# An eight-batch adaLN block on one core: the steps around the FFN's pairs put in another order

## The chip, the cores and the metric

The kernel runs on one core of a Trainium2 chip. The metric is the time of one execution on the device in microseconds (us); a lower one is better. A core has five engines that run side by side, each in the order of its own instructions: PE (TensorE, matrix products; its weight loads are shown apart as PEld), DVE (VectorE), ACT (ScalarE), POOL (GpSimd) and SP (SyncE, which here only issues DMAs). They wait for each other by semaphores. Every tile in PSUM that PE writes lies in a bank of its own out of a pool; a new tile waits until the last reader of the bank's previous tile is through.

## The reference

Everything is float32. x is 8 batches of 1024 rows of 256.

```python
mod = (_silu(L0_c) @ L0_wmod).reshape(L0_c.shape[0], 6, 1, -1)
sa, ca, ga, sb, cb, gb = (mod[:, 0], mod[:, 1], mod[:, 2], mod[:, 3], mod[:, 4], mod[:, 5])
ga = (2 * (ga >= 0) - 1) * jnp.maximum(jnp.abs(ga), 0.25)      # gb alike
h = _layernorm(x) * (1 + ca) + sa
x = x + ga * attn(h)       # softmax((h * w_lhs) @ (h * w_rhs).T) @ h
h = _layernorm(x) * (1 + cb) + sb
x = x + gb * (relu(h @ W1 + b1) @ W2 + b2)
```

## The kernel before

**Tiles and steps.** For each batch b there are eight steps i, one for each tile of 128 rows of queries. A step does part of batch b's attention and, in the same stretch, a part of the FFN of batch b-1 (its first half of 512 rows in steps 0 to 3, its second half in steps 4 to 7), of the preparation of batch b+1, and of the way back of finished FFN rows to memory. The order is written out by hand: the program pins every engine's instructions in the order in which the code issues them (`pin`, line 63), so a call that stands later in the loop stands later in the queue of every engine that it uses. Only a few POOL instructions go through a list (`later`, `spare`, lines 632 to 637).

**Attention.** `direct`(b, i) (line 403) makes row tile i of the scores on PE from `lT` and `rT`, the two scaled "sides" of the transposed input, and ACT copies it to `sc`. `mirror`(b, i) (424) fills the column block from the row block: DVE transposes 32x32 blocks into a tile `T`, and SP moves them through DRAM (`move`, 300: four writes of 32 partitions each to `D_m`, then one read). `row_max` (461) is DVE; `max_turn` (466) puts the maxima into a PSUM tile `pm` by PE; `subtract` (471) is DVE, `exponent` (483) ACT. The step works two tiles ahead: step i runs `direct` and `row_max` of `ahead` = tile i+2, and `subtract` and `exponent` of `late` = tile i+1.

Products with the values are made for pairs of tiles (i, i+1) with seven block products instead of eight. `pair_begin` (539) makes the first two on PE (tile `pp`, 16 products, 1.78 us), ACT copies half of it to `W` (one buffer); `pair_begin_sum` (558) is one addition on DVE; `left_sums` (563) are four on POOL, of 1.27 us; `pair_end` (574) makes the other five products into `pq` and `pr`, and `pair_out` (594) adds up and updates x on DVE, reading `W` last.

**FFN.** `ffn_rstd` (639) and `ffn_norm` (643) normalise on ACT into the single buffer `X`; `ffn_blocks` (676) turns it: two DVE transposes and a `move` (`D_f` written, `X_f` read); `ffn_turn` (682) applies scale and shift. The first layer goes by four pairs c of columns of W1, two in each of steps 0 and 1, or 4 and 5. Of a pair, `pair_products` (723) makes `pa`, `pb` and `pc` on PE and copies `pa` to `kept` on ACT, and in between calls `max_turn`; `pair_sums` (751) is five DVE instructions (L757, L760, L763, L766, L767); `pair_last` (769) is one more product into `pa`, an addition on DVE (L775) and one on POOL (L776); `pair_relu` (780) is two on ACT; `pair_turn` (787) four on POOL. The second layer is `y_first` (803) in steps 2 and 6 and `y_second` (825) in 3 and 7. In `y_first`, PE writes the first half of `ya` and of `yb`, ACT copies the first half of `ya` to `Y`, and PE goes on with the second halves in the same banks. `y_gate`, `y_turn`, `y_add` and `y_out` (846 to 878) scale, turn back through DRAM (`D_y`), add to x and store.

**PSUM.** `pa`, `pb`, `pc`, `pp`, `pq`, `pr`, `ya` to `yd` share four banks (pool `ps_a`); scores have two (`ps_s`), the turned maxima two (`ps_t`).

**The next batch.** `prepare_rstd` (269) and `prepare_norm` (272) normalise on ACT into `xg`; `prepare_blocks` (331) turns it (`D_a`, `X_a`); `prepare_turn_apart` (336) writes a side, `rT` (side 1) or `lT` (side 0), of one half of the rows, two ACT instructions each. `direct`(b+1, 0), the first PE work of step 6, needs `lT` of the first half and `rT` of both.

**SP.** All these moves and the stores are in one queue in the order of the code; the read of a move waits on SP until the writes have landed, and what is behind it waits too. The read of `y_turn` alone is put off behind the next move's read (`read_back`, 296).

The change is in the loop over the steps: in its branch `if first:` (lines 1208 to 1281; steps 0, 1, 4 and 5), in the part behind both branches (1341 to 1369), and in `middle` and `norms` (1106 to 1135).

Of the kernel before, what the change touches and what calls it, by code (L numbers as in the profile page):

```python
# [24 lines left out]
def adaln_block_kernel(  # L25
# [445 lines left out]
    def subtract(b, i):  # L471

        pm = pT_t.pop((b, i))
        pT = work.tile([P, NT, P], F32, tag="pT", name=f"pT_{b}_{i}")
        nc.vector.tensor_tensor(  # L475
            pT.rearrange("p j (a v) -> p j a v", v=V),
            score_columns(b, i),
            pm[:, :P].rearrange("p (j a v) -> p j a v", j=1, v=V).to_broadcast([P, NT, NV, V]),
            ALU.subtract,
        )  # L480
        pT_t[b, i] = pT

    def exponent(b, i):
        nc.scalar.activation(pT_t[b, i], pT_t[b, i], AF.Exp)  # L484
# [78 lines left out]
    def left_sums(b, i):  # L563


        s1 = two_t["s1"] = work.tile([P, TH, P], F32, tag="s1", name=f"s1_{b}_{i}", bufs=1)
        nc.gpsimd.tensor_tensor(s1, *halves(pT_t[b, i + 1]), ALU.add)  # L567
        (a11, a12), (a21, a22) = halves(pT_t[b, i]), halves(pT_t[b, i + 1])
        add = nc.gpsimd.tensor_tensor
        add(a21, a11, a21, ALU.subtract)  # L570
        add(a11, s1, a11, ALU.subtract)
        add(a12, a12, a11, ALU.subtract)
# [91 lines left out]
    def x_plus(b, g):  # L664

        for t in range(g * TH, (g + 1) * TH):
            xr = x_tile(b, t)
            later(xr, xr, rows_t[b][:, 1, :], ALU.add)
# [436 lines left out]

    def middle(b, i):

        if i == 0:
            ffn_norm(b - 1, 1)
        elif i == (6 if b < B - 1 else 5):  # L1110
            ffn_norm(b, 0)

    def norms(b, i):
        if b > 0 and i == 0:
            ffn_blocks(b - 1, 1)
        if b == 0:
            if i == 0:
                prepare_start(1)
        elif b + 1 < B:
            if i == 1:  # L1120
                prepare_start(b + 1)
                prepare_stats(b + 1, 0)
            elif i == 2:
                prepare_blocks(b + 1, 0)
                x_plus(b + 1, 0)
                xg_times(b + 1, 0)
        elif i == 5:

            ffn_blocks(b, 0)
        if b == B - 1:  # L1130
            return
        if i == 6:
            if b == 0:
                ffn_norm(b, 0)
            ffn_blocks(b, 0)
# [7 lines left out]
    for b in range(B):  # L1143
        for i in range(NT):
# [63 lines left out]
            if first:  # L1208

                ub, ug = (b - 1, 0) if i >= TH else (b - 2, 1)  # L1210
                back = i % TH == 0 and ub >= 0
                returned = i % TH == 1 and ub >= 0
                pair_products(fb, fg, c, turn_max)
                if i == 0:
                    ffn_rstd(b - 1, 1)
                if back:
                    y_gate(ub)
                if i == 4:
                    if b + 1 < B:
                        prepare_rstd(b + 1, 1)  # L1220
                if i == TH + 1:
                    pair_relu(c - 1)
                pair_sums(fb, fg, c)
                if (b, i) == (1, 0):
                    subtract(*late)
                if back:
                    y_turn(ub, ug)
                if ahead:
                    mirror(*ahead)
                if i % TH == 1:  # L1230
                    left_sums(b, i - 1)
                pair_last(fb, fg, c)
                if i % TH == 1:
                    pair_turn(c - 1)
                if (b, i) == (B - 1, 5):
                    pair_stats(b, 2)
                if late and i != 4 and (b, i) != (1, 0):
                    subtract(*late)
                pair_products(fb, fg, c + 1, (lambda: max_turn(*extra)) if extra else None)
                if (b, i) == (1, 0):  # L1240
                    exponent(*late)
                    late = None
                if (b, i) == (B - 1, 5):
                    ffn_rstd(b, 0)
                if i == 5:
                    exponent(*late)
                    if b + 1 < B:
                        prepare_turn_apart(b + 1, 1, 1)
                        prepare_turn_apart(b + 1, 1, 0)
                if i == 1:  # L1250
                    exponent(*late)
                elif i == 4 and b + 1 < B:
                    prepare_norm(b + 1, 1)
                    x_plus(b + 1, 1)
                pair_relu(c)
                sides_too = i == 4 and b + 1 < B
                if sides_too:
                    prepare_turn_apart(b + 1, 0, 1)
                if late and i == 0:
                    exponent(*late)  # L1260
                if sides_too:
                    prepare_turn_apart(b + 1, 0, 0)
                middle(b, i)
                pair_sums(fb, fg, c + 1)
                pair_last(fb, fg, c + 1)
                if i == 4:
                    if b + 1 < B:
                        prepare_blocks(b + 1, 1)
                        xg_times(b + 1, 1)
                    weights(*late)  # L1270
                if ahead and ahead != extra:
                    row_max(*ahead)
                if returned:
                    for q in range(2):
                        y_add(ub, ug, q)
                pair_turn(c)
                if i == 0:
                    pair_relu(c + 1)
                if c > 0:
                    pair_relu(c + 1)  # L1280
                    pair_turn(c + 1)
            else:
                half = i % TH - 2
                if i == NT - 2 and b < B - 1:
                    pair_stats(b, 2)
                if i == 2:
                    pair_begin(b, i)
                elif i == 3:
                    turn_max()
                elif i == 6:  # L1290
                    pair_begin(b, i, lambda: (max_turn(*late), weights(*late)))
                else:
                    turn_max()
                    pair_end(b, i - 1)
                    if not ahead:

                        pair_out(b, i - 1)
                        pair_stats(b, i - 1)
                if half:
                    y_second(fb, fg)  # L1300
                else:
                    y_first(fb, fg, turn_max if i == 2 else None)
                if ahead:
                    mirror(*ahead)
                if i == 2 and b + 1 < B:
                    prepare_rstd(b + 1, 0)
                elif i == 6 and b + 1 < B:
                    ffn_rstd(b, 0)
                elif i == NT - 1 and b == B - 1:
                    ffn_rstd(b, 1)  # L1310
                if not half:
                    pair_begin_sum(b, i)
                    if i == 2:
                        weights(*late)
                    left_sums(b, i)
                spare()
                early(b, i)
                if late and half:
                    weights(*late)
                middle(b, i)  # L1320
                if i == 2 and b + 1 < B:
                    load_x(b + 1, 1)
                spare()
                if ahead:
                    row_max(*ahead)
                if half:
                    if i == NT - 1 and ahead:
                        pair_out(b, i - 1)
                    y_second_sums(fb)
                    if i == NT - 1 and b == B - 1:  # L1330
                        y_gate(fb)
                    elif i == 3:
                        pair_stats(b, 0)
                        if b + 1 < B:
                            prepare_stats(b + 1, 1)
                else:
                    y_first_sums()
                    if i == NT - 2:
                        pair_stats(b, 4)
                spare()  # L1340
# [10 lines left out]
            if not first:  # L1351
                for _ in range(4 if half else 1):
                    spare()
            if i in (0, 4):
                pair_begin(b, i)
                pair_begin_sum(b, i)
            elif i in (1, 3, 5):
                pair_end(b, i - 1)
                pair_out(b, i - 1)
            elif i == NT - 1 and ahead:  # L1360
                pair_stats(b, i - 1)
            late = ahead if ahead != extra else None
# [82 lines left out]
```

## Time and profile before

| what | value |
|---|---|
| median of 3 runs | 794.17 us (793.29 to 794.22) |
| the profiled execution's own time | 792.67 us |
| span of its profile | 790.7 us |
| granted TensorE clock, mean | 0.996 |
| one batch (from step 2 to step 2, b=1 to 7) | 95.2, 94.8, 96.4, 95.0, 96.0, 95.1 us |
| of a batch, mean busy: PE, DVE, ACT, POOL | 91.8, 78.1, 47.6, 75.2 us |

The profile is of one execution; its times count from the span's start. The views used are the page (busy time of each engine), the waits (which instruction waited for whom), the timeline (instructions with start, duration, engine, line, operation, out<-in, shapes; in square brackets the idle time of the engine before it and what ended it) and the windows (busy time and clock in given stretches). A timeline line can stand for several instructions in a row (x4). PE's ends are modelled, so PE is read by its starts: a product of 256 columns starts 0.216 us after the one before it when nothing holds it up.

### The profile page before, as it was taken

To read this page: it belongs to the slowest core of one execution; us is meant where nothing else is said; L and a number is where in the kernel's file an instruction comes from. 1 tells how busy PE (TensorE), PEld (TensorE's weight loads), DVE (VectorE), ACT (ScalarE), POOL (GpSimd) and SP (SyncE) were. 2 spreads that over 40 slices of the span, in tenths; PEclk is the share of its full clock that TensorE was granted. 3 is DMA by queue.
4 is the path that set the end of the run, shared out by engine and by line. 5 is a ranking of instruction groups with operands and counts; after the bars stand their busy time and mean duration, and the time that the engine had idled before them with its cause. 6 is when DMAs were issued, how large, how long until landed. Compare 5 with 4: busy or idle time off the path is not lost.

```text
span 790.7 us, 12472 instructions
## 1 busy us (share of the span) xinstructions
PE 758.2 (96%) x4044; PEld 626.3 (79%) x4044; DVE 621.0 (79%) x1358; ACT 374.8 (47%) x695; POOL 576.9 (73%) x686
## 2 busy tenths in 40 slices
PE   8999998999989999899998999999998999989998
PEld 4687787787877788787787878878787877878887
DVE  7896988779886889768898788977888779686833
ACT  4563536534365534735346354553646535242521
POOL 3754776968869597895968959698696987759730
PEclk9999999999999999999999999999999999999999
DMA  8033433345544353444544444335453335224230
GB/s 295 15 108 113 127 105 96 104 135 158 144 114 127 111 173 103 114 128 124 177 110 118 147 147 128 97 110 167 132 149 91 114 116 154 74 61 147 56 104 27
DMA packets 106216, 95.25 MB, mean 120 GB/s; under 512 B 29700, under 2 KB 98848, under 8 KB 106152
## 3 DMA queue, kind: packets, MB, share of 16 engines
q1 hardware_dynamic: 98408, 85.81, 37.1%
q10 hardware_dynamic: 7744, 8.65, 3.4%
q8 instruction: 32, 0.52, 0.3%
q14 instruction: 32, 0.26, 0.1%
HBM read 50.62 MB, written 43.81 MB: 119 GB/s over the span
## 4 chain that ended last, share of the span: by engine, by line
PE 70%; DVE 13%; ACT 8%; issue 5%; DMA 3%; POOL 1%; SPq 0%; DVEq 0%; POOLq 0%; ACTq 0%
PE psc L412 14%; PE pr L588 8%; PE pq L588 7%; PE ya L799 6%; PE yc L799 6%; PE yb L799 6%; PE pa L721 4%; PE po L501 4%; PE pp L549 3%; PE pb L721 3%; PE yd L799 3%; DVE pT L475 2%; DVE f L760 2%; DVE u L757 2%; DVE u L767 2%
## 5 line engine op out<-in xcount | busy, mean ns | idle before, releaser
L412 PE MATMUL psc<-rT,lT 128*128 128x512 f32 (+3 forms) x384 | 134.7, 487 | 0.0
L776 POOL TENSOR_TENSOR f<-f,kept 128x256 f32<-128x256 f32 x64 | 48.5, 757 | 107.4 <-DVE f L766 107.4
L484 ACT ACTIVATE pT<-pT 128x1024 f32<-128x1024 f32 x64 | 67.7, 1058 | 92.8 <-DVE pT L475 92.8
L419 ACT COPY sc<-psc 128x512 f32<-128x512 f32 (+3 forms) x96 | 44.4, 477 | 127.3 <-PE psc L412 113.3
L475 DVE TENSOR_TENSOR pT<-sc,pm 128x1024 f32<-128x1024 f32 x64 | 77.0, 1204 | 30.6 <-PE pm L468 12.5
L412 PEld LDWEIGHTS psc<-rT,lT 128*128 128x128 f32 x384 | 66.0, 191 | 36.7 <-issue 26.1
L463 DVE TENSOR_REDUCE m<-sc 128x1 f32<-128x1024 f32 x64 | 77.3, 1208 | 2.4 <-ACT sc L419 1.8
L588 PE MATMUL pq<-tsum,pT 128*128 128x128 f32 (+1 forms) x448 | 60.4, 278 | 9.3 <-DVE f L760 9.3
L721 PE MATMUL pb<-hs,w1s 128*128 128x256 f32 x256 | 66.8, 384 | 0.7 <-POOL hs L711 0.6
L721 PE MATMUL pc<-hT,w 128*128 128x256 f32 x256 | 65.7, 379 | 0.0
L742 ACT COPY kept<-pa 128x512 f32<-128x512 f32 x64 | 37.5, 586 | 56.5 <-PE pa L721 56.5
L588 PEld LDWEIGHTS pq<-tsum,pT 128*128 128x128 f32 x448 | 54.5, 192 | 11.6 <-DVE f L760 11.6
L549 PEld LDWEIGHTS pp<-xg,pT 128*128 128x128 f32 x448 | 54.3, 192 | 10.2 <-issue 6.0
L549 PE MATMUL pp<-xg,pT 128*128 128x129 f32 x448 | 56.0, 276 | 0.9 <-DVE rs_f L650 0.2
L721 PEld LDWEIGHTS pb<-hs,w1s 128*128 128x128 f32 x256 | 49.1, 193 | 9.0 <-POOL hs L711 1.9
L637 POOL TENSOR_TENSOR x<-x,rows 128x256 f32<-128x256 f32 x64 | 44.5, 730 | 13.3 <-ACT rows L1015 10.2
L721 PEld LDWEIGHTS pc<-hT,w 128*128 128x128 f32 x256 | 48.6, 190 | 6.6
L757 DVE SCALAR_TENSOR_TENSOR u<-pb,cols,kept 128x256 f32<-128x256 f32 x64 | 30.5, 477 | 27.1 <-PE pb L721 21.0
L799 PE MATMUL yc<-f,w2s 128*128 128x256 f32 x224 | 50.7, 379 | 0.0
L782 ACT ACTIVATE f<-f 128x512 f32<-128x512 f32 x64 | 39.9, 623 | 21.1 <-DVE f L775 21.1
L721 PE MATMUL pa<-hT,w1s 128*128 128x256 f32 x128 | 39.5, 394 | 9.1 <-ACT kept L742 9.1
L567 POOL TENSOR_TENSOR s<-pT 128x512 f32<-128x512 f32 x28 | 35.7, 1274 | 16.7 <-ACT pT L484 16.7
(167 smaller groups left out, 1934.7 us busy)
## 6 DMA issues: line engine op xcount, KB each, us to landing
D_f<-T_f SPq DMA_DIRECT2D x60, 128.0 KB, 3.5
X_f<-D_f SPq DMA_DIRECT2D x15, 512.0 KB, 3.6
D_a<-T_a SPq DMA_DIRECT2D x56, 128.0 KB, 2.6
D_y<-T_y SPq DMA_DIRECT2D x56, 128.0 KB, 2.3
Y<-D_y SPq DMA_DIRECT2D x14, 512.0 KB, 4.5
out_dram<-x SPq DMA_DIRECT2D x14, 512.0 KB, 3.0
X_a<-D_a SPq DMA_DIRECT2D x13, 512.0 KB, 3.3
x<-in_L_attn_x_dram ACTq DMA_DIRECT2D x12, 512.0 KB, 3.7
```

Source lines behind the costliest of these rows:

```text
L412: nc.tensor.matmul(psc[:, : hi - lo], lhsT=lT_t[b, i // TH][:, k, ts(i % TH, P)], rhs=rT_t[b, n][:, k, lo - n * HALF : HALF], start=(k == ...
L419: nc.scalar.copy(score_row(b, i)[:, lo // V : hi // V, :], psc[:, : hi - lo].rearrange("p (n v) -> p n v", v=V),)
L463: nc.vector.tensor_reduce(m, score_row(b, i), AX.XY, ALU.max)
L475: nc.vector.tensor_tensor(pT.rearrange("p j (a v) -> p j a v", v=V), score_columns(b, i), pm[:, :P].rearrange("p (j a v) -> p j a v", j=1, ...
L484: nc.scalar.activation(pT_t[b, i], pT_t[b, i], AF.Exp)
L549: nc.tensor.matmul(out, lhsT=lhs[:, t, :], rhs=xg_t[b][:, h * TH + t, P : P + XS], start=(t == 0), stop=(t == TH - 1),)
L588: nc.tensor.matmul(out, lhsT=lhs[:, t, :], rhs=rhs[:, t, :], start=(t == 0), stop=(t == TH - 1),)
L637: queue.append(lambda: nc.gpsimd.tensor_tensor(out, in0, row, op))
L721: nc.tensor.matmul(out, lhsT=lhsT, rhs=rhs, start=True, stop=True)
L757: nc.vector.scalar_tensor_tensor(u, pb[:, lo], b1_col(c), kept[:, lo], ALU.add, ALU.add)
L776: nc.gpsimd.tensor_tensor(f[:, c + NH, hi], f[:, c + NH, hi], kept[:, hi], ALU.add)
L799: nc.tensor.matmul(out, lhsT=lhs(c), rhs=rhs(c), start=(c == 0), stop=(c == NH - 1))
```

## The change

- `ffn_norm`(b-1, 1) and `ffn_blocks`(b-1, 1), the second FFN half's normalising and turning, go from step 0 to step 1: the normalising behind both pairs' sums and the exponent, the turning ahead of the next batch's statistics.
- In steps 0, 1 and 5 `subtract` and `exponent` of the late tile, which stood ahead of the second pair's sums, stand behind them. In step 4 they come the other way, from behind everything to directly behind the first pair's sums (`subtract`) and the second pair's products (`exponent`).
- `pair_begin` and `pair_begin_sum` of tiles 4 and 5 go from the end of step 4 to its head, ahead of the FFN's products; in step 0 `pair_begin` stands ahead of the softmax steps, its sum stays at the end. `left_sums`(b, 4) goes from step 5 to step 4.
- The next batch's sides of the first half (four ACT instructions) go from step 4 to the end of step 3; those of the second half go in step 5 from the middle to behind the softmax steps.
- `pair_relu`(1) goes from the end of step 0 to step 1. In step 4 the next batch's turning stays ahead of the row maximum.

```diff
     def middle(b, i):
-        if i == 0:
+        if i == 1:
             ffn_norm(b - 1, 1)
...
     def norms(b, i):
-        if b > 0 and i == 0:
+        if b > 0 and i == 1:
             ffn_blocks(b - 1, 1)
...
+                if i == 4:
+                    pair_begin(b, i)
+                    pair_begin_sum(b, i)
                 pair_products(fb, fg, c, turn_max)
...
-                if i == TH + 1:
+                if i % TH == 1:
                     pair_relu(c - 1)
                 pair_sums(fb, fg, c)
                 if (b, i) == (1, 0):
+                    subtract(*late)
+                elif i == 4:
                     subtract(*late)
                 if back:
                     y_turn(ub, ug)
                 if ahead:
                     mirror(*ahead)
-                if i % TH == 1:
-                    left_sums(b, i - 1)
+                if i == 1:
+                    left_sums(b, 0)
                 pair_last(fb, fg, c)
...
-                if late and i != 4 and (b, i) != (1, 0):
-                    subtract(*late)
                 pair_products(fb, fg, c + 1, (lambda: max_turn(*extra)) if extra else None)
...
-                if i == 5:
+                if i == 4:
                     exponent(*late)
+                    left_sums(b, i)
                     if b + 1 < B:
-                        prepare_turn_apart(b + 1, 1, 1)
-                        prepare_turn_apart(b + 1, 1, 0)
-                if i == 1:
-                    exponent(*late)
-                elif i == 4 and b + 1 < B:
-                    prepare_norm(b + 1, 1)
-                    x_plus(b + 1, 1)
+                        prepare_norm(b + 1, 1)
+                        x_plus(b + 1, 1)
                 pair_relu(c)
-                sides_too = i == 4 and b + 1 < B
-                if sides_too:
-                    prepare_turn_apart(b + 1, 0, 1)
-                if late and i == 0:
-                    exponent(*late)
-                if sides_too:
-                    prepare_turn_apart(b + 1, 0, 0)
-                middle(b, i)
                 pair_sums(fb, fg, c + 1)
                 pair_last(fb, fg, c + 1)
-                if i == 4:
-                    if b + 1 < B:
-                        prepare_blocks(b + 1, 1)
-                        xg_times(b + 1, 1)
+                if i == 0:
+                    pair_begin(b, i)
+                if late and i != 4:
                     weights(*late)
+                if i == 5 and b + 1 < B:
+                    prepare_turn_apart(b + 1, 1, 1)
+                    prepare_turn_apart(b + 1, 1, 0)
+                middle(b, i)
+                if i == 4 and b + 1 < B:
+                    prepare_blocks(b + 1, 1)
+                    xg_times(b + 1, 1)
                 if ahead and ahead != extra:
                     row_max(*ahead)
...
                 pair_turn(c)
-                if i == 0:
-                    pair_relu(c + 1)
...
-            if i in (0, 4):
-                pair_begin(b, i)
+            if i == 0:
                 pair_begin_sum(b, i)
             elif i in (1, 3, 5):
                 pair_end(b, i - 1)
                 pair_out(b, i - 1)
+                if i == 3 and b + 1 < B:
+                    prepare_turn_apart(b + 1, 0, 1)
+                    prepare_turn_apart(b + 1, 0, 0)
```

## The prediction

> **What bounds it now.** First the page: TensorE (PE) is busy for 96% of the span, so only its gaps can be won.
>
> ```profile
> PE 758.2 (96%) x4044; PEld 626.3 (79%) x4044; DVE 621.0 (79%) x1358; ACT 374.8 (47%) x695; POOL 576.9 (73%) x686
> ```
>
> Then PE's own waits (line waited for, total us, times, longest): the waits that come back in every batch.
>
> ```profile
> PE pq L588 <- DVE f L760: 9.3, 12, 2.3
> PE pa L721 <- ACT kept L742: 9.1, 8, 1.4
> PE pm L468 <- DVE m L463: 4.5, 6, 0.8
> PE pr L588 <- DVE f L775: 1.9, 7, 0.3
> ```
>
> Then the timeline of batch b=4 (359.8 to 455); 2, 3, 5 and 6 repeat it, with periods of 94.8 to 96.6. All times below are its. The end of step 1 and the head of step 2:
>
> ```profile
> 376.34 1.43 DVE L767 TENSOR_TENSOR u<-kept,u 128x256 f32<-128x256 f32 x1
> ...
> 378.79 1.22 DVE L475 TENSOR_TENSOR pT<-sc,pm 128x1024 f32<-128x1024 f32 x1
> ...
> 380.98 1.16 PE L588 MATMUL pq<-tsum,pT 128*128 128x128 f32 x8 [1.00 <-DVE f L760]
> ...
> 388.95 0.27 ACT L555 COPY W<-pp 128x129 f32<-128x129 f32 x1 [1.79 <-DVE x L616]
> ```
>
> **Stage A.** The five products of `pair_end` last 5 x 0.89 (starts 381.98, 382.87). PE was through with pair 3 at 378.43 and could have ended at 382.89; it ended at 384.65. Lost: 1.76. `pq` takes the bank of pair 3's `pb`, whose reader L760 stands behind `subtract`(b,2).
>
> Steps 4 to 6:
>
> ```profile
> 412.45 1.75 SPq L306 DMA_DIRECT2D D_y<-T_y  x4
> ...
> 417.73 1.20 DVE L463 TENSOR_REDUCE m<-sc 128x1 f32<-128x1024 f32 x1
> ...
> 420.75 0.70 PE L721 MATMUL pa<-hT,w1s 128*128 128x256 f32 x2 [1.45 <-ACT kept L742]
> ...
> 425.29 0.34 SPq L309 DMA_DIRECT2D X_a<-D_a  x1
> ...
> 428.51 1.52 ACT L342 ACTIVATE rT<-X_a,sides 128x512 f32<-128x512 f32 x2 [2.87 <-DMA X_a<-D_a]
> ...
> 429.20 1.02 PE L412 MATMUL psc<-rT,lT 128*128 128x512 f32 x2
> ```
>
> **Stage B.** PE ends pair 2's `pc` at 418.07, waits for the row maximum (418.93), then for `kept` behind ACT's long queue: 2.7 lost; with 0.4 more at `pq` (425.52), 3.1. A last line matters later: `rT`(b+1,1) starts on ACT only when X_a lands, and is there (first half 429.23) 1.7 before PE wants it (second block of scores, 429.20 + 1.72 = 430.92). If A and B both vanished, six batches would give 6 x 4.9 = 29 us. That is the ceiling.
>
> **Stage A after the change.** In step 0 `subtract`(b,1) and the shift leave the place ahead of pair 1's sums, so these run 368.09 to 370.24 (2.15, as 369.28 to 371.43 before), then `subtract` 1.15, row maximum 1.13, W's sum. The turning of X_f (1.22) is gone from there: DVE stands ready at 373.2, and pair 2's sums start at 374.28, when `pb` is through, not 374.70. ACT: relu(0) to 369.3, W's copy, exponent 371.8 to 372.8 (it waits for `subtract`), score copies, `kept` by 374.0: ahead of its need, 374.97; if that 0.9 were gone, PE would wait as in B. relu(1), moved, lies between `kept` of pairs 2 and 3, where ACT was idle 1.86. `left_sums` starts on POOL at 373.7 instead of 374.87. L767 then meets POOL's L570 (375.03 to 376.30) and ends 0.28 behind it, 376.58; before, it sat through nearly all of an L570 (1.43). L775 of pair 2 ends 377.5: `pr` no longer waits. Pair 3's sums start at 377.5, L760 ends 378.5: `pq`, wanted at 379.32, no longer waits. **PE gains 1.76.**
>
> What is late next: `subtract`(b,2) now starts at 380.0 to 380.4 (L767 of pair 3 may meet POOL's L776), and what follows is one chain. To its exponent 1.26 (378.79, 380.05); the exponent to the normalising now queued behind it 0.96 (369.33, 370.29); that, 2.1 (2.06 and the signal); the two turnings on DVE, which waits for it and has the next batch's statistics and `pair_out` queued behind it, 1.22; statistics 2.13 (383.55, 385.68); `pair_out` 2.35 to its last product and 0.34 to 1.06 for that; W's copy and Y's copy 0.6. Sum 11.0 to 11.7: Y's copy ends at 391.0 to 392.1, and PE's second half of `ya` needs it. Before it started at 391.72. PE comes there at 390.0, so all of 1.76 is given back: **0, from -0.7 to +0.4 a batch.** SP: the D_f writes go behind mirror(b,3), whose writes start earlier (377.2); X_f lands near 394.9, wanted at 396.05; its read now holds up the output store and mirror(b,4) to 392 (389.38 before), landing 399, against `subtract`(b,4) at 398.75: 0.3 of DVE time, inside the 0.56 that it waits at 406.43. I cost it nothing; 1.2 if that cover is gone. The load of x on ACT's queue writes the buffer that this store reads, so it goes out near 395 instead of 393.47; ACT's engine is busy with xg to 396.2, and the data is wanted at 403.5: nothing. In b=7 there are no next statistics: the chain is 2.13 shorter and the 1.76 stay won.
>
> **Stage B after the change.** Next batch's first sides (4 x 0.71 on ACT) go to step 3's end: X_a(b+1,0) lands about 0.65 ahead of step 4's start, 406.23, so they end at 408.5; ACT was idle 6.27 there. W's copy needs the new `pp` (407.09 to 408.87) anyway: nothing; above 0.5 us of delay W's sum would hold up DVE. `pp` runs at the head instead of the end: PE's total is the same, but every `pb` of step 4 comes 1.78 later, pair 0's sums start at 410.87, not 409.09. DVE then has 2.04 sums, 1.15 `subtract`(b,5) (new ahead of the rest), 1.23 turning of Y, 0.19 mirror, 0.37, 2.4 sums (L767 now beside `left_sums`: 0.41 becomes up to 1.43), 0.34, 1.22 turning, 1.20 row maximum: 10.1, to 421.0. (The exponent and xg's normalising are through on ACT at 418.0, 0.5 ahead of DVE's turning; `left_sums` puts off L776 and so relu(1) to 421.9, and `kept` of pair 3 is wanted by 423.) PE reaches that maximum at 418.5 and goes on at 421.1; before, it went on at 420.75. So the wait on `kept` turns into a longer one on the maximum. The later wait on `pq` (0.4) goes, since `subtract`(b,6) is behind: `pair_end` ends at 429.2, as before: **0, from -0.4 to +1.0.**
>
> But the turning of Y starts 1.78 + 1.15 = 2.93 later, and SP works in order behind it: D_y, D_m, two reads, D_a, X_a. From D_y's issue to the start of `rT`(b+1,1) it took 15.20, 15.72, 15.34, 16.06, 15.64 and 17.02 in batches 1 to 6, with waits for landings all the way; the turning of xg (419.8) is ready long before its writes are due (422.9). So `rT`'s first half is there 2.93 + 15.83 + 0.77 = 19.53 after the old D_y; PE wants it at 18.47 (430.92 - 412.45). **Price: 0.5, 1.0, 0.6, 1.3, 0.9, 2.3 by batch, with 0.1 for each restart: +7.** In batches 3 and 5 (granted clock 0.98 in the windows by batch, 1.00 in the others) PE itself ran 1.8 and 1.2 slow just before: where that comes again, it covers 1.5 of this: **+6**. The ends are 0 (14.7 everywhere) and 14 (17.0 everywhere).
>
> The trace's rows for such transfers are 2.3 (D_y), 2.6 (D_a) and 3.3 (X_a) from issue to landing. [...]
>
> **Batch 7.** A gains 1.76. In B no next batch exists; the normalising for the FFN goes behind `subtract`(7,6) (711.4), and the chain of A without statistics but with `subtract`(7,7) and its exponent gives Y's copy at 722.8, where `ya` went on at 721.24: +1.55. Together -0.2.
>
> **Sum.** 0 (A) + 0 (B's head) + 6 (late `rT`) - 0.2 = +6 on the profiled execution's 792.67 (span 790.7 and 1.97 around it): 798.5. The median of the runs shown, 794.17, is 1.5 above it: **800.0**.
>
> **Rivals.**
> 1. **Faster: the transfer stays hidden.** Place: SP's sixth write in a row took 1.89 at 414.77 (0.43 is usual; in batch 7 all four D_m took 1.89 together). If the new moment has no such stall, X_a comes 1.4 sooner, the late `rT` costs 0.2 or less, and A's -0.3 and B's -0.4 remain: 6 x -0.7 = -4: 790. It decides once D_y to `rT` takes under 14.7. Against: no batch of 1 to 6 was below 15.2. Chance 0.26.
> 2. **Nothing in sum**: the change takes the waits away and hands them back one for one; half the late `rT` against A's -0.3: 794 +- 1.6. Chance 0.16.
> 3. **Slower still**: `left_sums` beside pair 1's sums makes the chains longer (A +0.4 a batch, 2 in all), and X_a needs batch 6's 17.0 each time (6 x 2.4 = 14): 794.2 + 16 = 810. Chance 0.13.
>
> The forecast, 796 to 804, has 0.45. The range 789.5 to 807 leaves out the better half of rival 1 and most of rival 3. A measurement of this kernel tells 0.2% (1.6 us) from no change: faster 0.26, same 0.16, slower 0.58.
>
> **What would show it.** Right: `pq` without its wait in step 1; a wait of DVE of near 2 us ahead of T_f in step 1; `ya` waiting for ACT's Y in step 2; `pm` waiting for the maximum in step 5; `psc` in step 6 waiting for `rT` 1 us or more; the period still 95 to 98. Wrong: `psc` unhindered and a period under 94, or `ya` unhindered in step 2 (then A's 1.76 is kept: 800 - 10.6 = 789).

## The result, and the profile after

The changed kernel takes 803.63 us (median of 4 runs, 801.43 to 805.02), beside 793.73 for the kernel before (4 runs, 791.95 to 794.22): a ratio of 1.0126, 95% interval 1.0098 to 1.0155, so 1.3% slower. The forecast was 800.0 with 789.5 to 807. The profiled execution took 801.43 us with a span of 799.3, 8.6 more than before.

First the page of the changed kernel, TensorE's busy time and the ended chain by engine, then its waits (line waited for, total us, times, longest):

```profile
PE 758.0 (95%) x4044; PEld 624.8 (78%) x4044; DVE 621.5 (78%) x1358; ACT 377.5 (47%) x695; POOL 577.4 (72%) x686
...
PE 71%; DVE 19%; issue 3%; ACT 3%; DMA 3%; DVEq 0%; SPq 0%; ACTq 0%
```

```profile
PE pm L468 <- DVE m L463: 18.6, 7, 2.9
PE yb L799 <- DVE pr L606: 7.0, 7, 1.7
PE pb L721 <- DVE f L760: 3.1, 6, 0.5
PE ya L799 <- ACT Y L811: 2.8, 2, 2.6
PE pa L721 <- DVE f L775: 2.4, 7, 0.5
```

PE, DVE and POOL do the same work (ACT 2.7 us more); the waits have changed hands. Those for `kept` (9.1) are gone, those at `pq` fell from 9.3 to 0.3; in their place PE waits 18.6 for the row maximum, once a batch, and 7.0 for `pair_out`'s L606, also once a batch.

The span can be cut at PE's first product of steps 2, 4 and 6 (the start of `psc` L412 in the timeline). Means of batches 1 to 6, us:

| stretch | before | after | difference | predicted |
|---|---|---|---|---|
| start to step 2 of batch 1 | 98.02 | 95.88 | -2.14 | -1.76 |
| step 2 to 4 | 21.57 | 23.30 | +1.73 | +1.76 (A given back) |
| step 4 to 6 | 23.39 | 24.96 | +1.57 | 0 (B's head) |
| step 6 to the next 2 | 50.48 | 48.71 | -1.77 | -1.76 (A) + 1.0 (late `rT`) |
| batch 7, step 2 to 4 | 21.57 | 21.58 | +0.01 | 0 |
| batch 7, step 4 to the end | 98.53 | 100.09 | +1.56 | +1.55 |

The differences add up: -2.14 + 6 x 1.53 + 0.01 + 1.56 = 8.6. Stage A came out as predicted; what was lost came in steps 4 to 6. The agreement in batch 7 is partly chance: `ya` goes on 2.61 later there, not 1.55, and what follows is 1.05 shorter, 0.61 of it a wait for `hs` (L711, an input of the FFN's first products, made by POOL) that went.

The timeline of the changed kernel at the end of step 1 and in step 2 of batch b=4, in the places shown of before:

```profile
383.37 0.97 DVE L767 TENSOR_TENSOR u<-kept,u 128x256 f32<-128x256 f32 x1
383.65 1.06 PE L588 MATMUL pq<-tsum,pT 128*128 128x128 f32 x8
...
384.79 1.21 DVE L475 TENSOR_TENSOR pT<-sc,pm 128x1024 f32<-128x1024 f32 x1
...
387.00 2.06 ACT L653 ACTIVATE X_f<-x,rs_f,rb 128x256 f32<-128x256 f32 x4
...
389.09 1.30 DVE L322 STREAM_TRANSPOSE T_f<-X_f 128x512 f32<-128x512 f32 x2 [1.40 <-ACT X_f L653]
...
393.24 0.30 DVE L606 TENSOR_TENSOR pr<-W,pq 128x128 f32<-128x128 f32 x1
...
393.60 1.99 PE L799 MATMUL yb<-f,w 128*128 128x256 f32 x8 [0.98 <-DVE pr L606]
...
395.20 0.27 ACT L555 COPY W<-pp 128x129 f32<-128x129 f32 x1 [4.63 <-DVE x L616]
395.36 0.38 ACT L811 COPY Y<-ya 128x256 f32<-128x256 f32 x1
...
395.79 1.99 PE L799 MATMUL ya<-ft,w2s 128*128 128x256 f32 x8
```

`pq` starts without a wait. Then the chain of the prediction can be read line by line: `subtract` (384.79), exponent, normalising (387.00), turning (389.09, DVE idle 1.40 before it), `pair_out`, whose L606 frees the bank that `yb` takes, W's and Y's copies. From `subtract`'s start to the end of Y's copy it is 10.95; 11.0 to 11.7 had been worked out.

Steps 4 to 6 of the same batch:

```profile
419.61 1.27 POOL L567 TENSOR_TENSOR s<-pT 128x512 f32<-128x512 f32 x1 [1.71 <-ACT pT L484]
419.69 1.75 SPq L306 DMA_DIRECT2D D_y<-T_y  x4
...
420.09 0.81 DVE L277 SCALAR_TENSOR_TENSOR rs<-mva,ra 128x4 f32<-128x4 f32 x1
...
422.31 1.28 POOL L571 TENSOR_TENSOR pT<-s,pT 128x512 f32<-128x512 f32 x1
422.45 1.41 DVE L767 TENSOR_TENSOR u<-kept,u 128x256 f32<-128x256 f32 x1
...
425.53 1.18 DVE L463 TENSOR_REDUCE m<-sc 128x1 f32<-128x1024 f32 x1
...
426.76 0.32 PE L468 MATMUL pm<-ident,m 128*128 128x128 f32 x1 [2.90 <-DVE m L463]
...
431.89 0.34 SPq L309 DMA_DIRECT2D X_a<-D_a  x1
...
434.84 2.74 PE L412 MATMUL psc<-rT,lT 128*128 128x512 f32 x6
435.31 1.52 ACT L342 ACTIVATE rT<-X_a,sides 128x512 f32<-128x512 f32 x2 [1.11 <-DMA X_a<-D_a]
```

The same two DVE instructions in the kernel before:

```profile
412.86 0.14 DVE L277 SCALAR_TENSOR_TENSOR rs<-mva,ra 128x4 f32<-128x4 f32 x1
...
414.55 0.41 DVE L767 TENSOR_TENSOR u<-kept,u 128x256 f32<-128x256 f32 x1
```

In the changed kernel they run beside POOL's `left_sums` and end 0.02 after L567 and 0.27 after L571: L277 (a tile of 128 x 4) takes 0.81 instead of 0.14, L767 1.41 instead of 0.41. The maximum ends 11.5 after pair 0's sums began (415.19), not 10.1, and PE waits 2.90 for it. `rT` starts 15.62 after D_y, near the 15.83 of the prediction (14.70, 14.51, 15.94, 15.62, 16.13 and 16.00 in batches 1 to 6), but PE itself now comes 1.47 later to step 6, and nothing waits for it: its second block is due at 434.84 + 1.72 = 436.56, the first half of `rT` is there at 436.1.

### The profile page after: what moved, and what is told of

It reads as the page before. It is cut to its first block, busy times and chain, and to the rows that moved or that the text cites. A ratio compares the mean times of both kernels' runs of the same rounds, so it can differ in the third digit from the quotient of the medians.

```text
span 799.3 us, 12434 instructions
## 1 busy us (share of the span) xinstructions
PE 758.0 (95%) x4044; PEld 624.8 (78%) x4044; DVE 621.5 (78%) x1358; ACT 377.5 (47%) x695; POOL 577.4 (72%) x686
## 4 chain that ended last, share of the span: by engine, by line
PE 71%; DVE 19%; issue 3%; ACT 3%; DMA 3%; DVEq 0%; SPq 0%; ACTq 0%
PE psc L412 13%; PE pr L588 7%; PE pa L721 6%; PE yc L799 6%; PE pb L721 5%; PE ya L799 5%; PE pq L588 5%; PE yb L799 5%; PE pp L549 4%; PE po L501 3%; PE py L909 3%; PE yd L799 3%; PE pc L721 3%; DVE u L767 2%; ACT X_f L653 2%
## 5 line engine op out<-in xcount | busy, mean ns | idle before, releaser
L412 PE MATMUL psc<-rT,lT 128*128 128x512 f32 (+3 forms) x384 | 134.8, 487 | 0.0
L776 POOL TENSOR_TENSOR f<-f,kept 128x256 f32<-128x256 f32 x64 | 49.3, 771 | 95.3 <-DVE f L766 74.4
L412 PEld LDWEIGHTS psc<-rT,lT 128*128 128x128 f32 x384 | 66.4, 191 | 37.3 <-issue 25.3
L567 POOL TENSOR_TENSOR s<-pT 128x512 f32<-128x512 f32 x28 | 35.6, 1270 | 33.4 <-ACT pT L484 33.4
L757 DVE SCALAR_TENSOR_TENSOR u<-pb,cols,kept 128x256 f32<-128x256 f32 x64 | 30.4, 475 | 31.6 <-PE pb L721 26.4
L782 ACT ACTIVATE f<-f 128x512 f32<-128x512 f32 x64 | 40.2, 628 | 22.7 <-DVE f L775 22.7
L783 ACT ACTIVATE f<-f 128x512 f32<-128x512 f32 x64 | 39.7, 621 | 17.4 <-POOL f L776 17.3
```

The lines of the kernel that those rows point to most:

```text
L412: nc.tensor.matmul(psc[:, : hi - lo], lhsT=lT_t[b, i // TH][:, k, ts(i % TH, P)], rhs=rT_t[b, n][:, k, lo - n * HALF : HALF], start=(k == ...
L776: nc.gpsimd.tensor_tensor(f[:, c + NH, hi], f[:, c + NH, hi], kept[:, hi], ALU.add)
L782: nc.scalar.activation(f[:, c, :], f[:, c, :], AF.Relu)
```

## The experiments

Two theories stood at the start. **Theory 1**: the loss is DVE's longer chain to the maximum of step 4 (`pp` and `subtract` ahead of it, POOL's sums beside it); stage A gives back what it gains; late transfers lie behind. **Rivals** put the loss into the transfers (`rT`, or the queue of SP) or into the parts of the change that only look like gains. Ratios are to the kernel before, with 95% intervals.

**Steps 0 and 1 alone** (on the kernel before; the rest of the change left out):

```diff
-        if i == 0:
+        if i == 1:
             ffn_norm(b - 1, 1)
...
-                if late and i != 4 and (b, i) != (1, 0):
+                if i == 5:
                     subtract(*late)
...
+                if late and i < 2:
+                    weights(*late)
+                if i < 2:
+                    middle(b, i)
```

> Steps 0 and 1 of the change alone, on the kernel before. Theory 1 (the loss is made in steps 4 and 5; in steps 0 and 1 the 1.76 us won at pq and pr come back as the waits of yb and ya): before +-2 us, 792 to 796; pq without its wait, yb waiting 1 us, ya 0.3, psc of the next batch unhindered. Theory 2 (the loss comes from the normalising that was moved behind the exponent in step 1): most of the +10 us, 800 or more.

Measured: 795.82 us, 1.0029 (1.0011 to 1.0046). Steps 6 to 2 took 48.97 and 2 to 4 23.33: -1.51 and +1.76 beside before. Stage A gains at `pq` and gives all of it back. The +2.3 us over the whole kernel lie in steps 4 to 6, which take 23.97 instead of 23.39.

**Steps 3, 4 and 5 alone** (the other half of the change):

```diff
+                if i == 4:
+                    pair_begin(b, i)
+                    pair_begin_sum(b, i)
                 pair_products(fb, fg, c, turn_max)
...
+                elif i == 4:
+                    subtract(*late)
...
+                if i == 3 and b + 1 < B:
+                    prepare_turn_apart(b + 1, 0, 1)
+                    prepare_turn_apart(b + 1, 0, 0)
```

> Steps 3, 4 and 5 of the change alone, on the kernel before. Theory 1: +8 to +10 us, 802 to 804, with pm waiting about 2.9 us for the row maximum in each of six batches, and the old waits of pq and pr in step 1 still there. Theory 2: within 2 us of before.

Measured: 804.99 us, 1.0140 (1.0117 to 1.0163), with the same 18.6 of waits for the maximum. This half makes the whole loss by itself; the two halves (0.0029 and 0.0140) don't quite add up to the change (0.0126).

**`left_sums` back in step 5** (on the changed kernel):

```diff
-                if i == 1:
-                    left_sums(b, 0)
+                if i % TH == 1:
+                    left_sums(b, i - 1)
...
                     exponent(*late)
-                    left_sums(b, i)
```

> The changed kernel with left_sums of tiles 4 and 5 back in step 5. If POOL's long instructions beside pair 1's sums made DVE's way to the row maximum longer: L277 0.14 instead of 0.81 us, L767 of pair 1 0.41 instead of 1.41, the wait of pm down from 2.9 to 1.5 us; then PE comes to psc 1.4 earlier and meets rT, which has 0.5 us to spare, so psc waits 0.9: -0.5 us a batch, 800. If rT doesn't bind then, -1.4 a batch: 795. If the place of pp alone made the wait: pm keeps 2.9 us, 803.

Measured: 800.96 us, 1.0104 (1.0079 to 1.0129). Its timeline in step 4, and two lines of its waits:

```profile
420.48 0.14 DVE L277 SCALAR_TENSOR_TENSOR rs<-mva,ra 128x4 f32<-128x4 f32 x1
...
422.17 0.42 DVE L767 TENSOR_TENSOR u<-kept,u 128x256 f32<-128x256 f32 x1
```

```profile
PE pm L468 <- DVE m L463: 12.1, 7, 1.9
...
PE psc L412 <- ACT rT L342: 2.3, 2, 1.4
```

Both DVE instructions have their short times back, the wait for the maximum shrinks by 6.5 in sum, steps 4 to 6 by 1.39 (24.96 to 23.57). But steps 6 to 2 grow by 1.32 (48.71 to 50.03): the wait for `rT` that had been hidden shows (2.3 in sum), and so does one of PE in step 0 for `hs` (L711, 2.5 in sum), which stands in POOL's queue. The total falls by 2.7 between the medians, 1.7 by the ratios, and the intervals of this run and of the changed kernel overlap.

**The FFN's turning behind the statistics in step 1** (on the changed kernel), to take the wait of `yb` away:

```diff
-        if b > 0 and i == 1:
-            ffn_blocks(b - 1, 1)
...
                 prepare_stats(b + 1, 0)
+                ffn_blocks(b - 1, 1)
```

> The changed kernel with the next batch's statistics ahead of the turning in step 1. If DVE's wait for the normalising (1.40 us) is what makes pair_out, and with it yb and ya in step 2, late: statistics fill the wait, yb and ya go on without their 1.25 and 0.36 us, -1.4 us a batch, 795 to 796. If yb and ya wait for something else: 803 as the changed kernel.

Measured: 814.82 us, 1.0266 (1.0242 to 1.0291): the expectation missed by some 19 us. The wait of `yb` is gone (steps 2 to 4 take 22.23), but steps 4 to 6 take 28.28, and the granted clock of the profiled execution was 0.985 (0.996 in that of the changed kernel). SP's lines and the subtraction of tile 4 in the timeline of this run:

```profile
396.53 1.75 SPq L306 DMA_DIRECT2D D_f<-T_f  x4
...
400.14 0.34 SPq L309 DMA_DIRECT2D X_f<-D_f  x1
...
401.00 3.73 SPq L306 DMA_DIRECT2D D_m<-Tm  x4
...
407.51 0.54 SPq L309 DMA_DIRECT2D sc<-D_m  x1
...
411.48 1.22 DVE L475 TENSOR_TENSOR pT<-sc,pm 128x1024 f32<-128x1024 f32 x1 [2.71 <-PE pr L588]
```

D_f written late makes its read late; SP stands at that read, and mirror(b,4)'s writes (3.73 instead of 1.75 to 2.5), its read and `subtract`(b,4) behind it all shift, at last `pair_out`(b,2), which holds a bank that step 4 needs (`pb` waits 4.7 in sum for L606). The last line names a product of PE; that the subtraction waited for the read of `sc`, issued 3.97 before it, is inferred: in the profile of the kernel before, the reads of `sc` took in the median, by size, 2.2 (64 KB) to 3.7 (384 and 448 KB) from issue to landing, 3.2 those of 192 KB, the size of this one. What was costed at nothing in the change (SP's order in step 2) is the next limit in this order.

**The row maximum ahead of the next batch's turning in step 4** (the changed kernel with `left_sums` back in step 5):

```diff
+                if ahead and ahead != extra:
+                    row_max(*ahead)
                 if i == 4 and b + 1 < B:
                     prepare_blocks(b + 1, 1)
                     xg_times(b + 1, 1)
-                if ahead and ahead != extra:
-                    row_max(*ahead)
```

> The changed kernel with left_sums back in step 5, as in the run with that alone, and with the row maximum of step 4 ahead of the next batch's turning (1.2 us). Theory R (rT is the next limit: X_a comes 15 to 16 us behind the turning of Y, whatever PE does): the wait of pm falls from 1.9 to 0.7 us, the wait of psc for rT grows by as much, to 2.2 us, and the time stays at 800 to 801. Theory M (the row maximum alone sets stage B): 1.2 us less a batch, 793 to 794.

Measured: 798.98 us, 1.0066 (1.0041 to 1.0091). The waits for the maximum fall from 12.1 to 5.0 in sum. Theory R had the transfers take all of that back, theory M (the maximum alone as the limit) nothing; the time lies between their ranges. Of the 7.1, 0.8 came back at `rT` (2.3 to 3.1) and 4.2 as waits for DVE's sums that had not been there (`pb` for L760 2.3, `pr` for L775 1.9).

**And `subtract`(b,5) behind the turning of Y** (the kernel of the last experiment), to start the transfers 1.15 earlier:

```diff
-                elif i == 4:
-                    subtract(*late)
...
                 if ahead:
                     mirror(*ahead)
+                if i == 4:
+                    subtract(*late)
```

> As the run with the maximum ahead of the turning, and with subtract of step 4 behind the turning of Y and the mirror, so that SP's queue starts 1.15 us earlier. Theory R: rT comes 1.15 us earlier and all of it is won: -1.15 us a batch against that run, 793 to 794. Theory M: no difference from that run.

Measured: 802.57 us, 1.0116 (1.0091 to 1.0141): a miss. D_y goes out 1.13 earlier (8.02 after step 4's start instead of 9.15), but `rT` starts between 0.8 earlier and 0.7 later, by batch. From this run's timeline:

```profile
417.82 1.75 SPq L306 DMA_DIRECT2D D_y<-T_y  x4
...
430.56 1.27 POOL L572 TENSOR_TENSOR pT<-pT 128x512 f32<-128x512 f32 x1
...
432.55 0.63 ACT L783 ACTIVATE f<-f 128x512 f32<-128x512 f32 x1 [4.78 <-POOL f L776]
...
434.03 1.51 ACT L342 ACTIVATE rT<-X_a,sides 128x512 f32<-128x512 f32 x2
```

D_y to `rT` is now 16.21 (14.41 to 15.83 in the run before it), and no idle time stands before `rT`: it no longer waits for X_a, but stands in ACT's queue behind a relu that waits 4.78 for POOL's L776, which stands behind the last of `left_sums`. The transfer's lateness had a second one under it. Why the total went up by 3.6 over the kernel of the last experiment, and not merely stayed, is only partly accounted for: steps 4 to 6 take 0.38 longer, 2.3 in six batches, and where PE's wait for `rT` (3.1 in sum) falls to 0.12 a batch, that for `hs` rises from 2.7 to 4.0 in sum; the rest stays open.

**The next batch's first sides in step 3, alone** (on the kernel before):

```diff
-                sides_too = i == 4 and b + 1 < B
-                if sides_too:
-                    prepare_turn_apart(b + 1, 0, 1)
...
-                if sides_too:
-                    prepare_turn_apart(b + 1, 0, 0)
...
+                if i == 3 and b + 1 < B:
+                    prepare_turn_apart(b + 1, 0, 1)
+                    prepare_turn_apart(b + 1, 0, 0)
```

> The kernel before with one part of the change: the next batch's first sides in step 3. If ACT's 2.8 us of sides ahead of the exponent and kept are what made PE wait for kept in step 5: that wait (1.45 us) goes, pm keeps its 0.9, rT is just in time: -1.6 us a batch, 783 to 785. If the mirror's or the maximum's chain takes the wait's place: 792 to 794.

Measured: 786.29 us, 0.9911 (0.9888 to 0.9933). The wait for `kept` falls from 9.1 to 3.1 in sum. One part of the change is worth 7 us.

**`subtract` and exponent behind pair 3's sums in step 1, alone** (on the kernel before; the FFN's normalising and turning stay in step 0):

```diff
-                if late and i != 4 and (b, i) != (1, 0):
+                if late and i not in (1, 4) and (b, i) != (1, 0):
                     subtract(*late)
...
                 pair_last(fb, fg, c + 1)
+                if i == 1:
+                    weights(*late)
```

> The kernel before with one part of the change: in step 1, and there alone, subtract and exponent behind pair 3's sums; the normalising stays in step 0. If the order of subtract and the sums made pq wait, and the moved normalising is what gave the gain back: pq's wait (1.0 us) goes, pr keeps 0.3, and yb and ya wait for nothing: -1.2 us a batch, 785 to 787. If DVE's chain to pair_out takes the gain back without the normalising too: 792 to 794.

Measured: 786.74 us, 0.9919 (0.9895 to 0.9943): another 6.4 us, with `pq`'s waits down from 9.3 in 12 to 2.5 in 2, and steps 2 to 4 at 21.68.

**Both of these** (the two diffs above together on the kernel before):

> The kernel before with two parts of the change alone: the next batch's first sides at the end of step 3, and in step 1 subtract and exponent behind pair 3's sums (normalising and turning for the FFN stay in step 0). Theory 1 (the two gains lie in different stretches, steps 4 and 5 and steps 1 and 2, and add up): 793.1 - 6.8 - 6.4 = 779.9, so 779 to 782, with the pq wait gone, the kept wait down to about 3 in all, and periods near 93. Rival (what one wins another wait gives back, the late rT or subtract(b,4) behind the transfers): 785 to 787, the better of the two alone, with a new wait of 1 us a batch at psc or pT.

Measured: 780.29 us (779.78 to 781.56, 5 runs), 0.9833 (0.9816 to 0.9849). They add up: 1.7% faster than before, and the fastest kernel of this study.

```profile
PE pm L468 <- DVE m L463: 5.4, 6, 0.9
PE pq L588 <- DVE f L760: 4.5, 7, 2.3
PE pa L721 <- ACT kept L742: 3.1, 8, 0.4
```

**`pair_begin` of tiles 4 and 5 back at the end of step 4** (the changed kernel with `left_sums` back in step 5):

```diff
-                if i == 4:
-                    pair_begin(b, i)
-                    pair_begin_sum(b, i)
                 pair_products(fb, fg, c, turn_max)
...
-            if i == 0:
+            if i in (0, 4):
+                if i == 4:
+                    pair_begin(b, i)
                 pair_begin_sum(b, i)
```

> The changed kernel with left_sums(b,4) back in step 5 (as in e3) and pair_begin and pair_begin_sum of tiles 4 and 5 back at the end of step 4. Theory 1 (the 1.78 us of pp at the head are what makes the maximum of step 4 late beyond PE's arrival, and the turning of Y with it): against e3, 800.96, some 6 x 1.3 to 6 x 1.7 come back: 791 to 794; the pm wait, 12.1 in all in e3, falls below 4, and the waits of psc on rT go. Rival (subtract(b,5) ahead of pair 1's sums alone makes it late, and pp's place matters little, since PE does the same work in sum): 799 to 801 with the pm wait still 8 or more.

Measured: 793.28 us, 1.0004 (0.9987 to 1.0021), 0.0100 below the kernel with `left_sums` alone put back: about 8 us. In its timeline:

```profile
414.66 2.05 PE L549 MATMUL pp<-xg,pT 128*128 128x129 f32 x16 [1.47 <-DVE f L775]
...
418.30 1.18 DVE L463 TENSOR_REDUCE m<-sc 128x1 f32<-128x1024 f32 x1
...
419.59 0.27 PE L468 MATMUL pm<-ident,m 128*128 128x128 f32 x1
...
429.56 1.52 ACT L342 ACTIVATE rT<-X_a,sides 128x512 f32<-128x512 f32 x2 [0.92 <-DMA X_a<-D_a]
...
430.43 1.98 PE L412 MATMUL psc<-rT,lT 128*128 128x512 f32 x4 [0.89 <-ACT rT L342]
```

The maximum is ready in time, as expected; `pp` waits 1.47 for L775 in its stead (8.8 in sum). One part of the expectation failed: the waits for `rT` did not go, they rose from 2.3 to 6.5, because PE now arrives on time. Steps 4 to 6 fall by 1.95 to 21.62, and the late `rT` of the prediction is seen uncovered, 0.89 here.

**And `subtract` and exponent of step 4 back behind everything** (the kernel of the last experiment):

```diff
-                elif i == 4:
-                    subtract(*late)
...
-                if i == 4:
-                    exponent(*late)
-                    if b + 1 < B:
+                if i == 4 and b + 1 < B:
...
                     xg_times(b + 1, 1)
+                if i == 4:
+                    weights(*late)
```

> As e10 (the changed kernel with pair_begin of 4 and 5 at the end of step 4 and left_sums in step 5, 793.28), and subtract and exponent of step 4 back behind everything. Theory 1 (subtract(b,5) ahead of pair 1's sums is what is still lost in steps 4 to 6: pp waits 1.5 us a batch for L775, psc 6.5 in all for rT): both waits go, 783 to 787. Rival (the maximum of step 4 or the exponent late for the pair's end takes their place): 791 to 794 with a new wait of 1 us a batch in steps 5 or 6.

Measured: 786.63 us, 0.9918 (0.9903 to 0.9934). `rT`'s wait is no longer in the list, and that of `pp` for L775 falls from 8.8 to 1.4. 7 us for this one move.

**The normalising added to the gain of step 1** (on the kernel with `subtract` and exponent behind pair 3's sums, 786.74):

```diff
-        if i == 0:
+        if i == 1:
             ffn_norm(b - 1, 1)
...
-        if b > 0 and i == 0:
+        if b > 0 and i == 1:
             ffn_blocks(b - 1, 1)
...
                     weights(*late)
+                    middle(b, i)
```

> As e8 (the kernel before with subtract and exponent of step 1 behind pair 3's sums, 786.74), and in addition the FFN's second normalising behind that exponent in step 1 and its turning in step 1 behind pair 3's sums; step 0's softmax and relu(1) stay as before. Theory 1 (the normalising and turning put between the exponent and pair_out are what gives the gain of e8 back): 794 to 797, as in e1 (795.82), with yb waiting for DVE L606 and ya for ACT's Y about 1 us a batch each. Rival (the price of e1 against e8 lies in step 0's other edits, subtract behind the sums and relu(1) moved): 786 to 789 with ya and yb unhindered.

Measured: 798.22 us, 1.0061 (1.0043 to 1.0079), 1.2 above the upper end of what was expected. Its waits:

```profile
PE yb L799 <- DVE pr L606: 8.9, 6, 1.7
...
PE ya L799 <- ACT Y L811: 0.4, 2, 0.2
```

The price of the normalising and turning in step 1 is 0.0142, 11 us, and most of it is paid at `yb`, which waits for L606 (8.9 in sum). `ya`, for which about 1 a batch had been expected, hardly waits; `yb` stands before it and takes the wait.

## Why the prediction came out as it did

**Stage A: right.** PE's gain (1.76 predicted, 1.77 a batch measured in the mean, 1.58 in batches 2, 4 and 5) is given back by one chain (1.73), and in batch 7 it is kept. The experiments show the two halves apart: -6.4 us without the normalising, and +11 for putting it and the turning into the chain. One detail was off: the chain is felt at `yb`, through L606 and the bank, before `ya` and Y. T_f's wait was 1.40, not near 2.

**SP in step 2: right that it costs nothing here.** `subtract`(b,4) waits 1.81 in the changed kernel, 3.07 after the read of its data was issued (that it waits for this read is inferred; the line names a product of PE). That is more than the 0.3 that had been counted, but PE does not wait between steps 2 and 4 for anything behind it; the run with the turning behind the statistics shows what it costs without cover.

**B's head: the step that failed.** "10.1, to 421.0 ... **0, from -0.4 to +1.0**" was 11.5 and +1.57. The mechanism, a wait for the maximum in place of that for `kept`, was right; two terms were mis-sized. The 0.37 for L775 and what stands behind it took 1.04 (L277 beside POOL's L567), and the 2.4 for pair 1's sums took 3.15 (L767 beside L571). The text had L767 at "up to 1.43" and put only 0.36 of that into the sum. That is 1.4 a batch, 8.5 us in six batches, and with `left_sums` back exactly these two go.

**Late `rT`: late as predicted, wrong in being added.** In batch 4, D_y came 3.07 later (2.93 predicted) and `rT` 15.62 behind it (15.48 in the mean of six, 15.83 taken); against a PE as early as before it would have been 1.0 late. Where other kernels let it show, it cost 3.1 in sum (the maximum early) or 6.5 (`pp` back, where PE too comes earlier), so the size of +6 is not settled. But PE was 1.47 late by then: the delays of two chains that meet at one point do not add, the longer one counts. In the sum, a term put at 0 measured 1.57 a batch and the term put at +6 measured nothing; that the total lay so near is luck. The sign that was named, `psc` waiting 1 us or more, did not appear in the changed kernel.

**Netting hid the parts.** B's head was costed as one sum, 0, and that is what made the change look like a shuffle. Apart, the sides in step 3 are worth -7, `subtract` early in step 4 costs 7, `pp` at the head 8, `left_sums` 2 (not separable from nothing). Down the ladder the ratios are 0.9918, 1.0004, 1.0104, 1.0126, from the kernel with all three put back to the full change. The chains of waits of the kernel before offered the first gain in plain sight (`kept`, 9.1).

**The rivals.** Faster (the transfer hidden): `rT` was hidden, but behind a new wait and not by a shorter transfer. The sign of this rival, D_y to `rT` under 14.7, came in batch 2 alone (14.51; 14.70 in batch 1). Slower still named `left_sums` beside pair 1's sums, and saw it at A's place instead of B's.

## What to carry to other kernels

Price each move of a joint change by itself before netting: here two of them were worth 13 us together, and the others gave more than that back. When two late chains end at the same engine, take the longer one, and expect the second to appear as soon as the first is mended. A moved instruction on POOL is costed by what it then runs beside on DVE, every small instruction counted (here 0.67 more for L277 and 1.00 for L767), not only by its own queue.

## What the runs showed of the hardware

**Two DVE instructions beside `left_sums` ended just after a POOL instruction.** In the changed kernel L277, on 128 x 4 numbers, took 0.81 and ended 0.02 after POOL's L567 (420.90 and 420.88); L767 took 1.41 and ended 0.27 after L571 (423.86 and 423.59); in batches 1 to 6 alike. With `left_sums` back in step 5 they took 0.14 and 0.42. Where L767 and L571 began within 0.03 of each other (89.48 and 89.45), L767 kept its 0.42 and L571 took 1.58 instead of 1.28. L757 and L760, which read a tile in PSUM and ran in between beside POOL's L570, kept their 0.47 and 0.48; all operands of L277 and L767 are in SBUF. In these rows the price goes by what was left of the POOL instruction (0.79 of L567, 1.14 of L571), not by the size of the DVE one: 0.67 for 128 x 4 numbers, 1.00 for 128 x 256. What holds them up is not shown.

**In some batches PE ran at half speed for 3.41 us behind its waits between steps 4 and 6.** The kernel before, steps 4 to 6 of batches 2 and 3 (columns: stretch, its length, busy time of each engine, then the granted clock, DMA):

```profile
214.84:237.82 22.98, 20.62 (x124) 18.29 (x123) 20.01 (x43) 14.75 (x27) 15.16 (x19) 1.00 0.38 104
309.66:333.90 24.24, 22.04 (x124) 19.39 (x123) 19.65 (x43) 16.40 (x29) 16.41 (x20) 0.93 0.36 98
```

In both PE waits about 0.76 and 1.45. In batch 3 the eight products after that start 0.43 apart instead of 0.216, for 3.4 us, and the stretch is 1.26 longer at a granted clock of 0.93. In the changed kernel batches 3 and 5 have such a half-speed stretch (steps 4 to 6 of batch 3 take 25.98 at a clock of 0.93, those of batch 4 24.44 at 1.00). In the two kernels with the sides in step 3 whose waits there are short (that part alone, and with step 1's softmax; `kept` 3.1 in sum in each) the granted clock of the profiled execution was 0.998.

The two half-speed stretches of the kernel before begin at 324.36 and 515.50, 56 times 3.41 apart, and last 3.41 each. In the rows below, the second is the 3.41 us ahead of the first of them, the third that stretch itself, and the first a window of batch 2, 28 times 3.41 ahead of the second row (length, PE's busy time, clock, DMA):

```profile
225.37:228.78 3.41, 1.81 (x8) 1.00 0.21 34
320.95:324.36 3.41, 1.21 (x6) 1.00 0.40 62
324.36:327.77 3.41, 3.41 (x9) 0.50 0.79 264
```

In batch 3 both waits fall into the window and PE is busy for 35% of it; in batch 2 the second runs over into the next, and it is 53%. Ahead of the other half-speed stretches of the two kernels' profiles PE was busy for 1.28 of 3.41 us (before, from 512.09), 0.98 and 1.39 (after, from 326.34 and 520.90); but 1.42 in the changed kernel from 616.47 was followed by a clock of 1.00. So the same two waits came with 1.26 more in one batch and with nothing more in another; that their place in such windows decides is the author's estimate from these rows. This is in the gains too: the granted clock was 0.989 to 0.998 (mean 0.994) in 17 executions of the kernel before and 0.998 to 1.000 with both gains, which by an estimate from these figures is two to three half-speed stretches fewer, some 3 of the 13 us.

**The issue of SP's writes took different times.** Four D_m writes took from 1.73 to 4.21 us to issue in the kernel before (49 groups, 32 of them under 2); in the kernel with the turning behind the statistics, 3.73 where they followed a read (400.14) and a store (400.52) at once.
